# Eight-row edge steps for the last image, its four branch products taken two chunks at a time, the steps beside them dealt out by cost, and the last output strip in halves

## The chip, the cores and the metric

The kernel runs on one core of a Trainium2 chip. The metric is the device time of one execution in microseconds. TensorE is called PE here (its weight load PEld), VectorE DVE, ScalarE ACT, GpSimd POOL, and SyncE, which only issues transfers, SP.

## What is computed

The input `x` has shape (4, 512, 64, 64) in float32. Two layers follow each other.

Layer 0 is a multi-scale linear attention. It makes query, key and value by 1x1 products, adds a copy that went through a 5x5 depthwise convolution, attends within groups of eight channels, projects back to 512 channels, scales and shifts, and adds `x`. Its result is called `y` here. Layer 1 works on `y`:

```
sobel = sqrt(conv(y, SX)**2 + conv(y, SY)**2 + 1e-8)
lap   = abs(conv(y, LAP))
diag  = max(abs(conv(y, D1)), abs(conv(y, D2)))
grad  = sqrt(sobel**2 + lap**2 + 1e-8)
ef    = gelu(scale * (w_branch[k] @ E[k]) + shift)    for the four maps E[k], 128 channels each
att   = sigmoid(w_att2 @ gelu(w_att1 @ mean(ef)))     the mean is over all pixels
z     = w_fuse @ (ef * att) + b
out   = gelu(layernorm over channels(z)) + y
```

The attention vector `att` of an image needs every `ef` of that image, so no fuse step of an image can start before its last branch product is through.

## The kernel before, in words

The images are worked on one after the other. Each image is cut into four groups of heads for layer 0, and the code for a group emits its steps from a list written out by hand. What is left of an image, called its stages, is written as three Python generators that emit a piece of work and then yield:

- `project_out` (lines 608 to 666): the final product of layer 0. For each of eight strips of 512 pixels and each of four chunks of 128 channels it loads `xr`, multiplies eight 128x512 tiles `hd` by weights `fold_sb` (L655), adds shift and `xr` on DVE (L660), and stores to `y` in DRAM. That is 32 y steps per image; a strip holds every fourth row of one half of the image, so the first 16 steps give the upper half of `y`.
- `edge_branches` (L668): for 16 strips `u` of four rows, and for two pairs of chunks, `edges` loads `win` (two chunks, six rows with the halo, on SP's queue), and makes the four maps with eleven DVE instructions (L696 to L722) and four on ACT (Square L709, Abs L713, Square L719, Sqrt L723). `branches` multiplies two of the four maps, over all four chunks, into one PSUM bank (L730, 256 columns each), and ACT takes each result through Gelu with a sum over pixels into `pool_sb` (L737) and stores it to `ef` in DRAM from its own queue (L742). `win` has two buffers, `maps` three, `dv` one.
- `fuse_out` (L754): loads the fuse weights and their channel means (`wf_sb`, `wf_mean`, L765 to L771), then the attention vector (L777 to L798), then eight strips `j` of 512 pixels. `fuse` multiplies one output chunk (four matmuls of 512 columns, L808), ACT squares it (L810), DVE adds the bias to make `z` (L812), POOL sums the squares (L815). `norm` of the strip before multiplies by ones to sum over channels (`var`, L819), takes root (L821) and reciprocal (L822), and for each chunk loads `yr` (L826, two buffers), multiplies (DVE L829), takes Gelu (ACT L830), adds `y` (POOL L833) and stores (SP, L834). `z` has six buffers.

PSUM has two sets of four banks: the tag `ps` for ordinary products, and `quad` for four banks at once.

The order of the work on PE is that of emission. On the other engines a scheduler orders instructions; each engine's queue, SP's included, then runs in order. While the images before the last are worked on, `advance` emits the stages of the image before in proportion to estimated costs. After the last group of image 3 (the last image) nothing of layer 0 is left, and lines 940 to 956 emit the rest: the beginning of image 3's fuse stage (weights), 16 y steps of image 3, then one step of a list `rest` for each yield of image 3's edge stage. `rest` holds the second half of image 3's y steps and, after it, image 2's fuse stage. Last comes image 3's own fuse stage:

```python
    next(fused)
    next(edged)
    next(projected)
    ...
    for _ in range(NCH * NJ // 2):
        next(projected)
    rest = [projected] + behind
    for n, _ in enumerate(edged):
        while rest and next(rest[0], None) is None:
            rest.pop(0)
    for stage in rest + [fused]:
        for _ in stage:
            pass
```

Of the kernel before, what the change touches and what calls it, by code (L numbers as in the profile page):

```python
# [8 lines left out]
F32 = mybir.dt.float32  # L9
# [58 lines left out]
WAIT_Y, WAIT_E, WAIT_F = 32.0, 16.0, 26.0  # L68

# [14 lines left out]
def conv_seq_kernel(  # L84
# [582 lines left out]
    def edge_branches(b, efs, pool_sb, side):  # L667

        y = ys[b % 2]
        with ExitStack() as stack:  # L670
# [3 lines left out]
            share = SHARE_E / (2 * NJ * 4)  # L674

            slot = (2, 0, 1, 3)
            run = WB * 4 - 2
            yield 0.0

            def edges(u, pair):  # L680

                win = pool.tile([P, 2, 6 * WB], F32, name="win", tag="win")
                nc.sync.dma_start(
                    out=win,
                    in_=y[2 * pair : 2 * pair + 2].rearrange("c p r w -> p c (r w)")[:, :, 4 * u * WB : (4 * u + 6) * WB],
                )
                above, mid, below = (win[:, :, n * WB : (n + 4) * WB] for n in range(3))
                maps = pool.tile([P, 4, 2, 4 * WB], F32, name="maps", tag="maps", bufs=3)
# [4 lines left out]
                dv = pool.tile([P, 2, 2, 4 * WB], F32, name="dv", tag="dv", bufs=1)  # L693
# [8 lines left out]
                half = 2 * 4 * WB  # L702
# [22 lines left out]

            def branches(u, ks, maps):
                ps = ps_tile("br")
                for n, k in enumerate(ks):
                    for c in range(NCH):
                        nc.tensor.matmul(  # L730
                            rows(ps)[:, 4 * n : 4 * n + 4, :], lhsT=wbr_sb[:, k, c, :],
                            rhs=rows(maps[c // 2][:, slot[k], c % 2, :], WB)[:, :, 0:W],
                            start=(c == 0), stop=(c == NCH - 1),
                        )
                o = pool.tile([P, 2, 256], F32, name="ef_o", tag="ef_o")
                for n, k in enumerate(ks):
                    nc.scalar.activation(  # L737
                        o[:, n, :], ps[:, 256 * n : 256 * n + 256], AF.Gelu,
                        bias=shift1[:, k : k + 1], scale=scale1[:, k : k + 1], accum_out=pool_sb[:, k, u : u + 1],
                    )  # L740
                step = ks[1] - ks[0]
                nc.scalar.dma_start(  # L742
                    out=efs[u // 2][:, ks[0] : ks[1] + 1 : step, 256 * (u % 2) : 256 * (u % 2) + 256], in_=o
                )

            held = []
            for u in range(2 * NJ + 1):
                first = [edges(u, 0)] if u < 2 * NJ else []
                yield share if u else share + WAIT_E
                if held:  # L750
                    branches(u - 1, (1, 2), held)
                    yield share
                    branches(u - 1, (0, 3), held)
                    yield share  # L754
                if first:
                    held = first + [edges(u, 1)]
                    yield share if u else share + WAIT_E

    def fuse_out(b, efs, pool_sb, side):

        y = ys[b % 2]
        with ExitStack() as stack:
# [42 lines left out]
            def fuse(c, ef, zs, total):  # L805
                ps = ps_tile("zps")
                for k in range(4):
                    nc.tensor.matmul(ps, lhsT=wf_sb[:, k, ts(c, P)], rhs=ef[k], start=(k == 0), stop=(k == 3))  # L808
                sq = total if c == 0 else pool.tile([P, 512], F32, name="sq", tag="sq", bufs=3)
                nc.scalar.activation(sq, ps, AF.Square, bias=fbias[:, c : c + 1])  # L810
                z = pool.tile([P, 512], F32, name="z", tag="z", bufs=6)
                nc.vector.tensor_scalar(z, ps, fbias[:, c : c + 1], None, ALU.add)  # L812
# [4 lines left out]
            def norm(j, zs, total):  # L817
                ps = ps_tile("var")
                nc.tensor.matmul(ps, lhsT=ones, rhs=total, start=True, stop=True)  # L819
                rstd = pool.tile([P, 512], F32, name="rstd", tag="rstd", bufs=1)  # L820
                nc.scalar.activation(rstd, ps, AF.Sqrt, bias=ln_eps, scale=1.0 / C)  # L821
                nc.vector.reciprocal(rstd, rstd)  # L822
                for c in range(NCH):
                    z = zs[c]
                    yr = pool.tile([P, 8 * WB], F32, name="yr", tag="yr")
                    nc.sync.dma_start(  # L826
                        out=yr, in_=y[c].rearrange("p r w -> p (r w)")[:, (8 * j + 1) * WB : (8 * j + 9) * WB]
# [6 lines left out]
                    nc.sync.dma_start(out=out[b, c, :, ts(j, 512)], in_=z)  # L834

            held = None
            for j in range(NJ + 1):
                if j < NJ:
                    ef = []
                    for k in range(4):  # L840
                        t = pool.tile([P, 512], F32, name="ef", tag="ef", bufs=8)
                        nc.sync.dma_start(out=t, in_=efs[j][:, k, :])
                        ef.append(t)
                    zs = []
                    total = pool.tile([P, 512], F32, name="total", tag="total")
                    fuse(0, ef, zs, total)
                    yield share
                    fuse(1, ef, zs, total)
# [3 lines left out]
                if held:  # L852
                    norm(j - 1, *held)
                    yield share
                if j < NJ:
                    fuse(2, ef, zs, total)
                    yield share
                    fuse(3, ef, zs, total)
                    yield share
                    held = zs, total  # L860

    def stages(b, heads, cheads, folded, side="right"):

        efs = [dram.tile([P, 4, 512], F32, name=f"ef{j}") for j in range(NJ)]
        pool_sb = small.tile([P, 4, 2 * NJ], F32, name="pool_sb")
# [75 lines left out]
    next(fused)  # L941
# [6 lines left out]
    for _ in range(NCH * NJ // 2):  # L948
        next(projected)
    rest = [projected] + behind  # L950
    for n, _ in enumerate(edged):
        while rest and next(rest[0], None) is None:
            rest.pop(0)
    for stage in rest + [fused]:
# [97 lines left out]
```

## Time and profile before

| what | value |
|---|---|
| median of three timed runs | 5082.15 us (5077.47 to 5088.09) |
| profiled execution, its own time | 5063.71 us |
| profiled execution, its span | 5061.9 us |
| mean granted PE clock | 0.967 |
| PE busy | 4702.0 us (93%) |
| DVE busy | 2124.7 us (42%) |
| ACT busy | 1626.5 us (32%) |
| POOL busy | 392.7 us (8%) |
| DMA | 866.26 MB, mean 171 GB/s |

The span runs from the first to the last instruction of one execution that was traced. The groups of instructions on the page are named by line, engine, operation and tile. A float32 matmul is two records on PE, so the 1024 products of a line appear as x2048. The landmarks in the last part of the trace are these: image 3's first y step starts at 4341 us, the first edge instruction of image 3 on DVE at 4452.83, the last y step ends shortly before 4594, the last branch product of image 3 ends at 4905.15, its first fuse product starts at 4910.71, and the last `var` product at 5038.01.

### The profile page before, as it was taken

The page shows a single profiled execution, that of the slowest core. Times are in us where ns is not written, and L with a number is a line of the kernel's source. Part 1 is how long each engine was busy: PE and PEld are TensorE (multiplying, and loading weights), DVE is VectorE, ACT ScalarE, POOL GpSimd, SP SyncE. Part 2 cuts the span into 40 slices and gives each one's busy share as a digit, 9 for nine tenths or more (in the row PEclk, how much of TensorE's full clock was granted, in tenths as well). Part 3 has the DMA queues.
Part 4 walks back from the last instruction along what each step waited for, and adds up shares of the span by engine and source line. Part 5 has one row for each costly group of instructions (what it writes and reads, how often), then busy time and mean ns, then how long its engine had stood idle before and what let it go on. Part 6 is the DMA issues. An engine that isn't in the chain of part 4 may idle for free. (4 is left out here: it accounts for less than half of the span.)

```text
span 5061.9 us, 107134 instructions
## 1 busy us (share of the span) xinstructions
PE 4702.0 (93%) x46362; PEld 2739.7 (54%) x46362; DVE 2124.7 (42%) x2960; ACT 1626.5 (32%) x2833; POOL 392.7 (8%) x291
## 2 busy tenths in 40 slices
PE   9999999999999999799899999899989898898777
PEld 5665654455666554454465655454456665445443
DVE  1222221116556433211455653431146557157965
ACT  2112111004444423200345442320024445035765
POOL 0000000000000013100000000310000000001335
PEclk9999999999999999899999999999999999999889
DMA  6444466666656565676555665657655553774425
GB/s 196 138 123 130 132 206 190 158 165 181 192 189 183 179 205 170 197 178 156 176 176 181 193 202 176 213 188 167 163 173 175 184 169 129 200 184 118 151 88 172
DMA packets 635945, 866.26 MB, mean 171 GB/s; under 512 B 324393, under 2 KB 395081, under 8 KB 617041
## 3 DMA queue, kind: packets, MB, share of 16 engines
q1 hardware_dynamic: 551504, 758.68, 51.8%
q10 hardware_dynamic: 83968, 100.74, 6.4%
q8 instruction: 364, 5.96, 0.5%
q14 instruction: 109, 0.88, 0.1%
HBM read 578.09 MB, written 213.98 MB: 156 GB/s over the span
## 5 line engine op out<-in xcount | busy, mean ns | idle before, releaser
L262 PE MATMUL proj<-xt,w_sb 128*128 128x512 f32 x2048 | 955.8, 610 | 52.9 <-DMA xt<-in_x 31.8
L655 PE MATMUL yps<-hd,fold_sb 128*128 128x512 f32 x2048 | 899.6, 596 | 9.7 <-DMA hd<-heads 8.7
L396 PE MATMUL cv<-inp,mat 32*32 32x512 f32 x20480 | 730.2, 597 | 35.4 <-issue 27.3
L262 PEld LDWEIGHTS proj<-xt,w_sb 128*128 128x128 f32 x2048 | 382.7, 194 | 523.3 <-issue 450.7
L655 PEld LDWEIGHTS yps<-hd,fold_sb 128*128 128x128 f32 x2048 | 384.9, 190 | 493.5 <-issue 445.3
L396 PEld LDWEIGHTS cv<-inp,mat 32*32 32x32 f32 x20480 | 420.3, 103 | 314.6 <-issue 154.2
L730 PE MATMUL br<-maps,wbr_sb 128*128 128x256 f32 x2048 | 495.0, 396 | 51.8 <-ACT maps L713 42.2
L808 PE MATMUL zps<-ef,wf_sb 128*128 128x512 f32 x1024 | 469.9, 610 | 53.5 <-DMA ef<-ef 19.0
L730 PEld LDWEIGHTS br<-maps,wbr_sb 128*128 128x128 f32 x2048 | 399.7, 198 | 165.9 <-issue 51.3
L284 PEld LDWEIGHTS val<-w_sb,xt 128*128 128x128 f32 x4096 | 470.2, 192 | 33.9 <-issue 26.1
L284 PE MATMUL val<-w_sb,xt 128*128 128x128 f32 x4096 | 484.9, 277 | 0.6 <-DVE vt L291 0.3
L660 DVE SCALAR_TENSOR_TENSOR yt<-yps,shift,xr 128x512 f32<-128x512 f32 x128 | 96.1, 750 | 871.8 <-PE yps L655 788.9
L268 ACT COPY strip<-proj 128x512 f32<-128x512 f32 x256 | 149.1, 582 | 928.5 <-PE proj L262 910.4
L451 PE MATMUL corr<-near,ckt 128*32 128x160 f32 x8192 | 333.6, 315 | 35.0 <-DMA near<-near 28.4
L808 PEld LDWEIGHTS zps<-ef,wf_sb 128*128 128x128 f32 x1024 | 196.1, 195 | 296.6 <-issue 235.6
L241 POOL TENSOR_TENSOR mat<-dp_sb 128x1280 f32<-128x1280 f32 x32 | 77.2, 2414 | 3464.5 <-PE cv L396 2951.0
L451 PEld LDWEIGHTS corr<-near,ckt 128*32 128x32 f32 x8192 | 256.9, 111 | 131.5 <-issue 73.1
L703 DVE TENSOR_TENSOR maps<-dv 128x1054 f32<-128x1054 f32 x128 | 162.6, 1271 | 366.9 <-PE br L730 366.9
L312 ACT ACTIVATE kt<-tr 128x512 f32<-128x512 f32 x128 | 75.8, 593 | 528.9 <-PE tr L310 345.9
L737 ACT ACTIVATE ef_o<-br,shift,scale 128x256 f32<-128x256 f32 x256 | 142.3, 559 | 283.5 <-PE br L730 251.9
L360 DVE RECIPROCAL rec<-rec 128x512 f32<-128x512 f32 x64 | 214.4, 3350 | 1.7
L812 DVE TENSOR_SCALAR z<-zps,fbias 128x512 f32<-128x512 f32 x128 | 94.9, 744 | 283.4 <-DMA out<-z 97.0
(125 smaller groups left out, 4135.7 us busy)
## 6 DMA issues: line engine op xcount, KB each, us to landing
xt<-in_x SPq DMA_DIRECT2D x316, 512.0 KB
near<-near SPq DMA_DIRECT2D x512, 264.0 KB
inp<-strip ACTq DMA_DIRECT2D x1024, 64.0 KB
win<-y SPq DMA_DIRECT2D x128, 396.0 KB
near<-vt SPq DMA_DIRECT2D x512, 66.0 KB
y<-yt SPq DMA_DIRECT2D x128, 264.0 KB
yr<-y SPq DMA_DIRECT2D x128, 264.0 KB
heads<-q SPq DMA_DIRECT2D x128, 256.0 KB
```

Of the source, the lines that this page charges most:

```text
L262: nc.tensor.matmul(ps, lhsT=self.w[t][:, c, :], rhs=xs[self.b, j][c], start=(c == 0), stop=(c == NCH - 1))
L268: nc.scalar.copy(s, ps)
L284: nc.tensor.matmul(ps[:, ts(c, P)], lhsT=xs[self.b, j][n][:, ts(c, P)], rhs=self.w[VALUE][:, n, :], start=(n == 0), stop=(n == NCH - 1),)
L360: nc.vector.reciprocal(rec, rec)
L396: nc.tensor.matmul(rows(banks[i])[32 * j : 32 * j + 32, :, c0:c1], lhsT=self.mat[t][q, j, (dx + 2) * 8 + 4 * b : (dx + 2) * 8 + 4 * b + 4, :],
L451: nc.tensor.matmul(self.banks[jj][32 * i : 32 * i + 32, 160 * b : 160 * b + 160], lhsT=self.held["c", i][:, at : at + 32], rhs=v[:, 4 * n ...
L655: nc.tensor.matmul(ps, lhsT=fold_sb[g // NG][:, g % NG, ts(c, P)], rhs=hd[g], start=(g == 0), stop=(g == 2 * NG - 1),)
L660: nc.vector.scalar_tensor_tensor(yt[:, :, 1 : W + 1], rows(ps), shift0[:, c : c + 1], rows(xr), ALU.add, ALU.add)
L703: nc.vector.tensor_sub(flat[:, half : 3 * half - 2], dvs[:, 2 : 2 * half], dvs[:, 0 : 2 * half - 2])
L730: nc.tensor.matmul(rows(ps)[:, 4 * n : 4 * n + 4, :], lhsT=wbr_sb[:, k, c, :], rhs=rows(maps[c // 2][:, slot[k], c % 2, :], WB)[:, :, 0:W] ...
L737: nc.scalar.activation(o[:, n, :], ps[:, 256 * n : 256 * n + 256], AF.Gelu, bias=shift1[:, k : k + 1], scale=scale1[:, k : k + 1], accum_o ...
L808: nc.tensor.matmul(ps, lhsT=wf_sb[:, k, ts(c, P)], rhs=ef[k], start=(k == 0), stop=(k == 3))
```

## The change

The change touches only what is emitted after the last group, and the three stage generators.

1. For image 3 (`side == "left"`) the edge stage takes eight rows per strip: eight strips, two pairs of chunks each, 16 calls of `edges` with tiles twice as long. After each call its pair of chunks is multiplied at once: for all four maps, two chunks each, 512 columns, into four banks of the tag `quad`; the second pair of a strip closes the sums, and then ACT makes four Gelus of 512 columns and stores them in two transfers. The order on PE is: emit `edges(n)`, then other steps, then the products of `edges(n-1)`.
2. The other steps are dealt out by cost: each y step counts 6.9 us and each fuse step 2.95, and each pair of chunks is followed by 34 us of them the first time and an even share (11.76 us) afterwards; 18 us are kept for the time in which image 3's attention vector is made.
3. Image 2's attention vector is made among the first 16 y steps of image 3 (after steps 5, 9 and 13). Image 3's fuse weights are loaded when its y steps are through, not before them.
4. Image 2's `z` (b == B - 2) is made by ACT, not by DVE.
5. The last strip of image 3's fuse stage is worked on as two pieces of 256 pixels.

The rest of the diff only passes lengths through (`tall`, `wide`, `n`, `piece`) so that other images keep their four-row steps. Its core:

```diff
+            tall = 8 if side == "left" else 4
+            steps, wide = H // tall, tall * W
...
+            def product(ps, k, c, maps):
+                nc.tensor.matmul(
+                    rows(ps), lhsT=wbr_sb[:, k, c, :], rhs=rows(maps[:, slot[k], c % 2, :], WB)[:, :, 0:W],
+                    start=(c == 0), stop=(c == NCH - 1),
+                )
+
+            def store(u, ks, parts):
+                o = pool.tile([P, 2, wide], F32, name="ef_o", tag="ef_o")
+                for n, k in enumerate(ks):
+                    nc.scalar.activation(
+                        o[:, n, :], parts[n], AF.Gelu,
+                        bias=shift1[:, k : k + 1], scale=scale1[:, k : k + 1], accum_out=pool_sb[:, k, u : u + 1],
+                    )
+                at, step = wide * u % 512, ks[1] - ks[0]
+                nc.scalar.dma_start(out=efs[wide * u // 512][:, ks[0] : ks[1] + 1 : step, at : at + wide], in_=o)
...
+            if side == "left":
+
+                banks = None
+                for n in range(2 * steps + 1):
+                    made = edges(n // 2, n % 2) if n < 2 * steps else None
+                    yield 1.0
+                    if n:
+                        u, pair = divmod(n - 1, 2)
+                        if pair == 0:
+                            banks = quad_tiles("br")
+                        for k in (1, 2, 0, 3):
+                            for c in (2 * pair, 2 * pair + 1):
+                                product(banks[k], k, c, held)
+                        if pair:
+                            for ks in ((1, 2), (0, 3)):
+                                store(u, ks, [banks[k] for k in ks])
+                    held = made
+                yield 0.0
+                return
...
+            pieces = [(j, 0, 512) for j in range(NJ)]
+            if b == B - 1:
+                pieces[-1:] = [(NJ - 1, 0, 256), (NJ - 1, 256, 512)]
...
-                nc.vector.tensor_scalar(z, ps, fbias[:, c : c + 1], None, ALU.add)
+                z = pool.tile([P, 512], F32, name="z", tag="z", bufs=6)[:, :n]
+                if b == B - 2:
+                    nc.scalar.activation(z, ps, AF.Identity, bias=fbias[:, c : c + 1])
+                else:
+                    nc.vector.tensor_scalar(z, ps, fbias[:, c : c + 1], None, ALU.add)
...
-    next(fused)
     next(edged)
     next(projected)
...
-    for _ in range(NCH * NJ // 2):
+    for n in range(NCH * NJ // 2):
         next(projected)
-    rest = [projected] + behind
-    for n, _ in enumerate(edged):
-        while rest and next(rest[0], None) is None:
-            rest.pop(0)
-    for stage in rest + [fused]:
+        if n in (4, 8, 12):
+            next(behind[0])
+    rest, spent, given = [projected] + behind, 0.0, 0.0
+
+    def fill(much):
+
+        nonlocal spent, given
+        given += much
+        while rest and spent < given:
+            spent += FILL_Y if rest[0] is projected else FILL_F
+            if next(rest[0], None) is None:
+                if rest.pop(0) is projected:
+                    next(fused)
+
+
+    each = FILL_FIRST
+    for more in edged:
+        if not more:
+            break
+        fill(each)
+        each = FILL_EACH
+    for _ in range(3):
+        next(fused)
+        fill(FILL_ATT / 3)
+    for stage in rest + [fused, edged]:
         for _ in stage:
             pass
```

## The prediction

> **What bounds the kernel now.** I read first the engine rows in 40 slices of the page, where PE is full for most of the span and falls off in the last slices while DVE fills:
>
> ```profile
> PE   9999999999999999799899999899989898898777
> DVE  1222221116556433211455653431146557157965
> ```
>
> The chain of waits holds only the last 9 us, so I cut the end of the span into stretches: image 3's second half of y with its first edge strips (4459:4607), the remaining edge strips beside image 2's fuse steps (4607:4880), the drain and the attention vector (4880:4911), image 3's fuse steps (4911:5035), and the tail. Columns: length, then busy us and instruction count of PE, PEld, DVE, ACT, POOL, then clock, DMA share, GB/s.
>
> ```profile
> 4459.00:4607.00 148.00, 144.16 (x411) 77.38 (x410) 85.12 (x127) 62.90 (x84) 0.00 (x0) 0.98 0.68 166
> 4607.00:4880.00 273.00, 212.05 (x598) 124.47 (x598) 253.97 (x300) 202.66 (x277) 89.67 (x52) 0.89 0.41 127
> 4880.00:4911.00 31.00, 16.56 (x65) 13.48 (x64) 13.86 (x18) 21.26 (x33) 5.22 (x4) 0.72 0.25 85
> 4911.00:5035.00 124.00, 119.59 (x270) 50.72 (x269) 67.08 (x64) 59.84 (x75) 59.86 (x47) 0.99 0.49 153
> ```
>
> The first stretch is bound by PE (144 of 148) with DVE idle for 63 us; the second by DVE (254 of 273) with PE idle for 61; the third is a drain. The waits of PE from 4459 to 4911 say for whom (total, times, longest):
>
> ```profile
> PE br L730 <- ACT maps L713: 42.2, 8, 11.4
> PE zps L808 <- DVE z L812: 12.2, 3, 7.3
> PE zps L808 <- DVE wf_sb L797: 6.6, 2, 5.4
> ```
>
> The last link is named ACT, but behind the maps stands the full DVE. So one stage wastes DVE and the next wastes PE.
>
> **Prices.** In the PE timeline the matmuls run back to back:
>
> ```profile
> 4714.03 3.62 PE L730 MATMUL br<-maps,wbr_sb 128*128 128x256 f32 x16
> 4717.48 10.46 PE L808 MATMUL zps<-ef,wf_sb 128*128 128x512 f32 x24
> ```
>
> A 128x512 record costs 0.434 us (3.60 us to the next start for 8), a 128x256 one 0.226; every f32 matmul is two records. So a y step (8 matmuls) is 6.95 us, a fuse step (4) 3.48, its `var` 0.87, eight br matmuls of 512 columns 6.95. On DVE I take start-to-start times, since a duration overlaps the next start:
>
> ```profile
> 4712.19 1.25 DVE L703 TENSOR_TENSOR maps<-dv 128x1054 f32<-128x1054 f32 x1
> 4713.36 0.69 DVE L706 SCALAR_TENSOR_TENSOR maps<-win,maps 128x524 f32<-128x524 f32 x1
> 4713.98 0.69 DVE L717 TENSOR_TENSOR maps<-dv 128x526 f32<-128x526 f32 x1
> ```
>
> That is 1.17 us for 1054 elements and 0.62 for 524: 1.04 ns per element and 0.07 fixed. ACT the same way: 0.97 for 1048 elements, 0.53 for 524, so 1.85 for 2096, and 2.05 for the Sqrt.
>
> **Part 1, eight-row edge steps.** Before: 32 half steps of 10 x 0.62 + 1.17 = 7.35 us of DVE. After: 16 steps of 10 x 1.17 + 2.26 = 13.9. That saves 0.8 x 16 = 12 us of DVE, no more: the fixed cost is small. The br matmuls go from 512 records of 256 columns (138.1 us busy in the trace, 116 if dense) to 256 of 512 columns, 111 us. ACT per step: 0.97 + 1.85 + 1.85 + 2.05 = 6.7, and half as many table switches. Loads of `win` and stores of `ef` halve in number on SP's and ACT's queues; the bytes of `win` shrink with the halo.
>
> Against this speaks the Trainium skill (Perfetto Trace Analysis, Optimizing Scalar/DVE Operations): where Scalar or Vector is not saturated but causes bubbles on others, break instructions up. By it, the 5.3 us mean wait of PE for maps would double: if all 8 waits stay, 42 us more, over half of the gain that follows. But in the stretch where those waits are, DVE is busy 93%, so the condition does not hold; the larger step is filled over on PE (part 2). I take nothing, and keep 42 us for a rival.
>
> **Part 2, products at once, other steps dealt out.** The product of each pair of chunks needs one pair's maps. It accumulates in four banks of its own, a new wait: the first product of a strip waits for the previous strip's four Gelus on ACT (one Gelu 0.78 us, a table load 1.29), and behind it on PE stand the fuse steps. In the built order 11.8 us of fill stands between (except once, between products 5 and 6, where maps are old); nothing up to 11.8 us, the excess beyond. The fills are 5 y steps, then 2, 2, 2, 1, 2, 2, 0, then about four fuse steps each.
>
> PE from T0 = 4459, the end of the 16th y step (its eviction starts at 4459.06): 16 x 6.95 = 111 of y, 16 x 6.95 = 111 of br, 120 of image 2's 128 fuse matmuls x 0.87 = 104, six `var` 5; sum 332. That is PE's bound for the end of the last product.
>
> DVE: edge step n needs one of three `maps` buffers, so product n-3 done. Adding up PE's order, products 4 and 5 end at T0+132 and +153. Step 7 thus runs T0+132 to 146; step 8 starts at 146 and waits 3.5 us for a buffer. From there: 8 x 13.9 = 111; five of image 2's norms, which stand ahead of the last edge step in the built order, 5 x (3.34 + 4 x 0.87) = 34 (L822's mean, and L829's 0.96 in that stretch less the overlap); the weight mean of `next(fused)`, now in mid-stage, 2048 elements, 2.1; contention with POOL. For the last: the 21 half steps of the second stretch cost (254 - 75.5 of L812, L829, L822, L797)/21 = 8.5 instead of 7.35, 24 us by 52 POOL instructions; 35 of these give 16. Sum 163; at the 254 of 273 that DVE reached before, 175. So DVE ends at T0+146+3.5+175 = +324.5. The last step's exposed ACT square 3, Sqrt with table load 3.3, product 7: T0+338, 4797. DVE and PE are now nearly level; before, that product ended at 4905.
>
> **Part 3, z of image 2 on ACT.** It takes 32 x 0.66 = 21 us off DVE (L812's 0.73 less the overlap; already left out above) and puts 30 x 0.57 = 17, the pace of L810, on ACT in the late half. ACT there: 8 x 6.7 + 20 Gelus x 0.78 + 60 evictions x 0.57 + 6 x 0.58 + 24 x 0.71 + 14 table loads (counted in the built order) x 1.29 = 142 us of some 185. The page ScalarE: Activation LUTs (What ACT_TABLE_LOAD costs) speaks against it: each switch 1283 ns and a drain of 1380. The row shows the load, and the next activation 1.29 us after its start:
>
> ```profile
> 4713.60 1.28 ACT L737 ACT_TABLE_LOAD   x1
> 4714.89 0.56 ACT L737 ACTIVATE ef_o<-br,shift,scale 128x256 f32<-128x256 f32 x1
> ```
>
> So no drain beyond it is seen. By the page ACT would need 142 + 14 x 1.38 = 161 us, still under 185. I take 142. Queued behind a waiting zps eviction on ACT are the next edge activations; four banks, 14 us of PE work, cover that.
>
> **Part 4, attention steps.** Image 2's two small products (0.63 + 1.05 us in the trace at 4597) move before T0, among y steps: +2 us on T0; the 5.4 us wait for `wf_sb` and the ones beside it go (PE is the bound there afterwards, counted in the 332). Image 3's weights load (1.3 MB on SP) moves from the start to after the last y store, ahead of the second `win` of the fifth strip; that win is needed only after DVE's 14 us of step 8: nothing, 0 to 6. Image 3's attention chain: product end to first zps was 4910.71 - 4905.15 = 5.6 us; now image 2's last two fuse steps lie in it (7.8 us), and its last norms stand before Sigmoid on DVE and ACT; I take 16 (12 to 22).
>
> First zps: 4813, 98 us before 4910.7.
>
> **Part 5, last strip in halves.** PE +0.5. The tail hangs on SP and two `yr` buffers:
>
> ```profile
> 5026.93 1.13 PE L819 MATMUL var<-total,ones 128*128 128x512 f32 x2 [0.46 <-DVE z L812]
> ...
> 5053.18 0.92 SPq L826 DMA_DIRECT2D yr<-y  x2
> 5056.55 2.30 POOL L833 TENSOR_TENSOR z<-z,yr 128x512 f32<-128x512 f32 x2 [3.78 <-issue]
> ```
>
> Each pair of chunks costs one round of load (3.4 us) and POOL (2.3). Halving shortens the reciprocal by 1.7, POOL by 1.2 per pair, and DVE and ACT by about 2, but adds a norm, so two more rounds of about 4 us, and z's six buffers wait for stores of the strip before. Gain 5, loss 5 to 8: I take 1.5 us lost, from -6 to +8.
>
> **Sum.** 98 - 2 - 1.5 = 94 us. The profiled span 5061.9 becomes 4968; its execution took 5063.71 (1.8 us around the span), so 4970. The median of the three timed runs is 5082.15, 18 above; I subtract the same 94: **4988**.
>
> **Rivals.**
> - *PE alone bounds* (0.15): DVE loses nothing to waits, the product ends at the 332, six us earlier, and the tail gains 6 where I took a loss of 1.5: about 4975. For it: PE's clock was 0.89 in the second stretch and 0.98 to 0.99 where it is full. Against: three engines at 77 to 95% seldom mesh.
> - *The bubbles stay* (0.17): each late step still costs PE the 5.3 us that a wait for maps costs now, 8 x 5.3 = 42: 5030. For it: ACT's strict order mixes edges, evictions and Gelus. Against: a step now has a fill of 11.8.
> - *Slower* (0.05): the four br banks become the lock. If the Gelus of a strip stand on ACT behind all of the next edge step, and the evictions with them, PE idles a DVE step of about 22 us less one product of 7 per strip: 8 x 15 = 120 us lost, 5108. It decides from 94/8 = 11.8 us per strip on. Against: in the built order the Gelus follow one Sqrt at most.
> - The balance as worked out: 0.63.
>
> **How the numbers follow.** The measurement tells about 0.2% (10 us) from no change. Range 4966 to 5032: the first rival, part 5's gain, the ends of parts 4 and 5 below and above, and the 42 us. Only a loss of over 84 us makes it "same": 0.02 between bubble and lock. Faster 0.94, slower 0.04.
>
> **What would show it.** DVE in the second half of image 3's edges busy over 90% beside PE over 85% at a clock near 1; br 256 records, about 111 us; DVE's edge steps near 14 us before POOL works and 16 after; waits of br for maps under 25 us; the first zps of image 3 near 4813; the tail from the last full `var` longer than 35 us. I am wrong if br waits long for `ef_o` Gelus, or ACT passes 90% there.

## The result, and the profile after

The changed kernel takes 5020.18 us (median of four runs, 5005.83 to 5033.35) against 5080.17 (5077.47 to 5088.09): ratio 0.988, 95% interval 0.9867 to 0.9893. The gain is 60 us; 94 were predicted. The time lies inside the range, 32 us above the number.

The profiled execution is the slowest of the four: 5033.35 us, span 5031.6. It reaches image 3's first y step at 4362.7, before's at 4341.4, although the code up to there does the same work; over the thirteen kernels traced after the change the point lies between 4338.0 and 4365.2. So stages are counted from that y step, called y0 below. From y0 to the end: 720.5 us before, 668.9 after.

| us from y0 | before | after | term of the sum |
|---|---|---|---|
| PE ends the 16th y step (T0) | 116.5 | 123.9 | 117.6 + 2 predicted, 4.3 late |
| first edge product starts | 139.0 | 178.4 | |
| last edge product ends | 563.8 | 494.8 | T0+338 predicted, T0+370.9 |
| image 3's first fuse step | 569.3 | 509.0 | 16 us later predicted, 14.3 |
| end | 720.5 | 668.9 | 152.7 us later predicted, 159.8 |

The prediction took for T0 the start of that step's eviction on DVE, 1.1 us behind PE's end. The misses are 4.3 + 32.9 - 1.7 + 7.1 = 42.6 us, which to 0.2 us is the difference between 94 and 51.6.

PE and DVE in 40 slices, from the page of the changed kernel:

```profile
PE   9999999999999999799899999989999899899887
DVE  1222222115565533311355553441125555447955
```

The hole in the last slices of PE is smaller, and DVE's block is shorter. The same stretches as before, cut at the changed kernel's own points: from T0 to the first late fill, the late half of the edges, the attention vector, image 3's fuse steps, and the tail. Columns: length, then busy us and count of PE, PEld, DVE, ACT, POOL, then clock, DMA share, GB/s.

```profile
4486.00:4643.00 157.00, 152.87 (x352) 66.56 (x351) 124.33 (x106) 71.72 (x59) 0.00 (x0) 0.99 0.62 153
4643.00:4858.00 215.00, 191.71 (x418) 82.25 (x417) 178.15 (x117) 147.66 (x179) 85.91 (x46) 0.93 0.48 155
4858.00:4872.00 14.00, 10.32 (x36) 4.84 (x35) 7.13 (x10) 10.21 (x15) 4.81 (x4) 0.91 0.20 75
4872.00:4991.00 119.00, 109.39 (x253) 48.01 (x254) 69.39 (x65) 64.72 (x82) 63.83 (x50) 0.97 0.57 175
4991.00:5032.00 41.00, 16.92 (x54) 12.24 (x54) 18.17 (x24) 17.96 (x26) 16.97 (x19) 0.71 0.43 129
```

In the first stretch DVE now works 124 of 157 us beside a full PE; before it idled there for 63 of 148. In the second no engine is full: PE 89%, DVE 83%, ACT 69%. The waits of PE over both (total, times, longest):

```profile
PE var L864 <- ACT z L853: 16.0, 3, 7.4
PE var L864 <- POOL total L858: 5.4, 1, 5.4
PE yps L661 <- DMA hd<-heads: 4.1, 2, 3.7
PE zps L848 <- ACT z L853: 1.9, 3, 1.2
```

The 42.2 us of `br` waiting for maps are gone. In their place stand 21.4 us at `var`, the small product with which a fuse strip makes its variance (before the change it waited 3.4 us there). Beside them PE's own work is 344.6 us busy where 332 were reckoned (br 116.1 for 256 records, y 113.8, zps 109.2, `var` 11.0; they overlap a little). 344.6 + 27.4 idle = 372. Part of the excess is slow work right behind a wait: the four `var` that waited take 2.05 to 2.08 us, the two that did not 1.02.

A `var` needs two things. One is the strip's sum of squares, which ACT and then POOL make. The other is a free bank of the tag `ps`: there are four, and a strip takes five in turn (four `zps`, one `var`). ACT empties a bank by taking the square and `z` from it. `var` reads no `z`, so the row "`var` <- ACT z", 16.0 of the 21.4 us, is a wait for a bank. PE, ACT and POOL around the second of the four waits (start, us, engine, line, operation; idle before and its releaser in brackets):

```profile
4763.92 2.08 PE L864 MATMUL var<-total,ones 128*128 128x512 f32 x2 [3.91 <-ACT z L853]
```

```profile
4758.76 2.93 ACT L876 ACTIVATE z<-z,vec_sb 128x512 f32<-128x512 f32 x4
...
4763.18 0.69 ACT L853 ACTIVATE z<-zps,fbias 128x512 f32<-128x512 f32 x1 [0.16 <-DMA out<-z]
```

```profile
4751.52 2.62 POOL L858 TENSOR_TENSOR total<-total,sq 128x512 f32<-128x512 f32 x2 [12.82 <-ACT sq L850]
```

The sums were through at 4754.14. The `z` that empties the bank stood on ACT behind four Gelus, waited 0.16 us for the store of an earlier `z`, and ended at 4763.87; `var` starts at 4763.92. At 4795.51 it is the same; at 4707.45 sum and `z` end within 1 us of each other. Only the last of the four waits, 5.40 us, is for the sum. The timelines of PE and ACT around it:

```profile
4809.98 10.46 PE L848 MATMUL zps<-ef,wf_sb 128*128 128x512 f32 x24
4825.84 2.07 PE L864 MATMUL var<-total,ones 128*128 128x512 f32 x2 [5.40 <-POOL total L858]
4827.71 9.19 PE L738 MATMUL br<-maps,wbr_sb 128*128 128x512 f32 x16
4836.74 13.90 PE L848 MATMUL zps<-ef,wf_sb 128*128 128x512 f32 x32
4850.47 7.03 PE L738 MATMUL br<-maps,wbr_sb 128*128 128x512 f32 x16
```

```profile
4818.02 1.08 ACT L720 ACTIVATE lap<-maps 128x1052 f32<-128x1052 f32 x1
...
4819.14 1.96 ACT L724 ACTIVATE maps<-maps 128x2104 f32<-128x2104 f32 x1
4821.00 1.94 ACT L730 ACTIVATE maps<-maps 128x2104 f32<-128x2104 f32 x1
4822.85 0.67 ACT L850 ACTIVATE sq<-zps,fbias 128x512 f32<-128x512 f32 x1
```

PE has the last of the strip's `zps` ready at 4820.4. Its square stands on ACT behind 5 us of an edge step's activations and starts at 4822.85; POOL's last sum follows, from 4823.65 to 4825.8, and `var` starts at 4825.84. All that stands behind `var` on PE is late with it: the product of step 14, then 14 us of fill, then the last product at 4850.47. DVE's last edge instruction had begun at 4824.70 and ended at 4826.9, 23.6 us before that product began. The prediction put 6.3 there.

### The profile page after: what moved, and what is told of

The parts are those of the page before. It is cut to its first block, busy times and chain, and to the rows that moved or that the text cites. A ratio compares the mean times of both kernels' runs of the same rounds, so it can differ in the third digit from the quotient of the medians.

```text
span 5031.6 us, 106279 instructions
## 1 busy us (share of the span) xinstructions
PE 4694.3 (93%) x46140; PEld 2689.2 (53%) x46140; DVE 2083.3 (41%) x2761; ACT 1581.8 (31%) x2712; POOL 397.3 (8%) x298
## 5 line engine op out<-in xcount | busy, mean ns | idle before, releaser
L661 PE MATMUL yps<-hd,fold_sb 128*128 128x512 f32 x2048 | 907.8, 599 | 18.5 <-DMA hd<-heads 16.2
L848 PE MATMUL zps<-ef,wf_sb 128*128 128x512 f32 (+1 forms) x1056 | 473.4, 601 | 36.4 <-DMA ef<-ef 19.4
L738 PE MATMUL br<-maps,wbr_sb 128*128 128x256 f32 (+1 forms) x1792 | 474.2, 418 | 3.7 <-DVE s_sb L335 2.9
L738 PEld LDWEIGHTS br<-maps,wbr_sb 128*128 128x128 f32 x1792 | 340.9, 193 | 146.9 <-issue 102.0
L457 PE MATMUL corr<-near,ckt 128*32 128x160 f32 x8192 | 333.7, 315 | 40.3 <-DMA near<-near 32.9
L714 DVE TENSOR_TENSOR maps<-dv 128x1054 f32<-128x1054 f32 (+1 forms) x112 | 158.0, 1411 | 376.3 <-PE br L738 376.2
L746 ACT ACTIVATE ef_o<-br,shift,scale 128x256 f32<-128x256 f32 (+1 forms) x224 | 131.4, 590 | 228.1 <-PE br L738 210.4
L415 ACT ACTIVATE co<-cv 128x256 f32<-128x256 f32 x256 | 94.0, 398 | 331.1 <-PE cv L402 310.6
```

What stands on the lines that cost most here:

```text
L457: nc.tensor.matmul(self.banks[jj][32 * i : 32 * i + 32, 160 * b : 160 * b + 160], lhsT=self.held["c", i][:, at : at + 32], rhs=v[:, 4 * n ...
L661: nc.tensor.matmul(ps, lhsT=fold_sb[g // NG][:, g % NG, ts(c, P)], rhs=hd[g], start=(g == 0), stop=(g == 2 * NG - 1),)
L714: nc.vector.tensor_sub(flat[:, half : 3 * half - 2], dvs[:, 2 : 2 * half], dvs[:, 0 : 2 * half - 2])
L738: nc.tensor.matmul(rows(ps), lhsT=wbr_sb[:, k, c, :], rhs=rows(maps[:, slot[k], c % 2, :], WB)[:, :, 0:W], start=(c == 0), stop=(c == NCH ...
L746: nc.scalar.activation(o[:, n, :], parts[n], AF.Gelu, bias=shift1[:, k : k + 1], scale=scale1[:, k : k + 1], accum_out=pool_sb[:, k, u : u ...
```

## The experiments

All of them are edits of the changed kernel, run once each, e12 five times; the numbers are us from y0 of each run's own trace.

| run | last product ends | image 3's first fuse step | end | from there to the end |
|---|---|---|---|---|
| changed kernel | 494.8 | 509.0 | 668.9 | 159.8 |
| e1_z8_image2 | 489.7 | 504.5 | 662.2 | 157.7 |
| e2_z_on_dve | 488.8 | 504.1 | 663.9 | 159.7 |
| e3_last_strip_whole | 488.7 | 502.9 | 655.0 | 152.0 |
| e4_four_rows | 493.9 | 506.7 | 675.6 | 168.8 |
| e5_four_per_step | 527.9 | 532.8 | 691.0 | 158.2 |
| e6_z8_yr4_image2 | 489.1 | 504.7 | 663.7 | 159.0 |
| e7_no_sums_image2 | 470.9 | 486.7 | 645.6 | 158.9 |
| e8_first_fill_20 | 493.2 | 507.5 | 665.8 | 158.2 |
| e9_fewer_dve | 482.7 | 497.0 | 654.5 | 157.5 |
| e10_no_late_fill | 466.7 | 479.5 | 660.5 | 181.0 |
| e11_tail_buffers | 483.8 | 498.1 | 639.9 | 141.8 |
| e12_together | 466.6 | 479.5 | 649.6 | 170.2 |

e3 and e11 run the changed kernel's order up to image 3's first fuse step, and end the last product at 488.7 and 483.8; so 484 to 495 is what that order gives, and smaller differences in this column say nothing. Counted from the first product instead of y0, most of the spread goes: that stretch takes 316.4 us in the changed kernel, 314.0 in e3, 314.3 in e11.

### Dealing out, row height, halves and z, each undone

**e5_four_per_step.** The other steps four at a time again:

```
-        given += much
-        while rest and spent < given:
-            spent += FILL_Y if rest[0] is projected else FILL_F
-            if next(rest[0], None) is None:
+        for _ in range(4):
+            if rest and next(rest[0], None) is None:
```

Expected:

> The changed kernel with the dealing by cost undone: after each eight-row half step four of the other steps are emitted, whatever they cost, which is what the kernel before did (one after each of its yields). The y steps are then through after four half steps and image 2's fuse steps begin there. Theory (dealing out carries the gain): PE full and DVE waiting first, DVE full and PE waiting later, as before the change; last br product 530 to 550 us after the first y step of image 3, where the changed kernel in the runs so far has 489 to 495. Rival (the products two chunks at a time carry it, since PE no longer needs both pairs of maps): 490 to 505.

Measured: last product 527.9, 33 to 39 us later than in the changed kernel, e1, e2 and e6 (7 of them are two more fuse steps that stand ahead of it), and the end 22 to 29. The total is 5050.40 (before on this chip: 5068.72). Dealing out carries about half of the 52 to 58 us that lie between these ends and before's 720.5. The late stretch (from 4617 to 4886) is again as full of DVE as before the change:

```profile
4617.00:4886.00 269.00, 219.19 (x481) 94.27 (x479) 247.90 (x160) 190.81 (x224) 109.77 (x56) 0.90 0.45 145
```

DVE is busy for 248 of 269 us. PE waits 27.7 us at `var` and 21.1 at `br`; the other steps are used up at 4834, and the last two edge products wait 11.1 us and, in two halves, 5.7 and 4.3, with nothing left to fill.

**e4_four_rows.** Four-row edge steps with everything else kept:

```
-            tall = 8 if side == "left" else 4
+            tall = 4
```

Expected:

> The changed kernel with four-row steps for image 3 too, all else as changed: 16 strips, br products of 256 columns, the shares of the other steps halved. Theory: the rows are the small part: 12 us more of DVE and 5 of PE, last br product 5 to 20 us later than 494.6 after the first y step of image 3. Rival 1 (eight rows carry the gain): 40 us or more later. Rival 2 (the shorter step lets PE and ACT mesh better): earlier.

Measured: last product 493.9, end 675.6, total 5024.79. Beside e1, e2 and e6 (663.3 on average) eight rows are worth 12 us at the end. The last products can't be compared: with the shares halved, 28 of image 2's fuse steps stand ahead of it here and 30 there. In the late stretch, from 4640 to 4850, `br` waits again for maps, and now for its banks:

```profile
PE br L738 <- ACT ef_o L746: 15.0, 4, 7.9
PE br L738 <- ACT maps L734: 11.9, 3, 6.2
PE var L864 <- ACT z L853: 7.9, 2, 4.0
```

So the 12 us are not just the 12 us of DVE time that was reckoned; that the two agree may be chance.

**e2_z_on_dve.** Image 2's z on DVE again:

```
-                if b == B - 2:
-                    nc.scalar.activation(z, ps, AF.Identity, bias=fbias[:, c : c + 1])
-                else:
-                    nc.vector.tensor_scalar(z, ps, fbias[:, c : c + 1], None, ALU.add)
+                nc.vector.tensor_scalar(z, ps, fbias[:, c : c + 1], None, ALU.add)
```

Expected:

> The changed kernel with image 2's z made by DVE, as before the change (part 3 undone). Theory: DVE has 21 us more in a half where it is busy 90%, and the wait for z's stores now stands in DVE's queue ahead of edge instructions; the last br product ends 10 to 25 us later than the 494.6 us after the first y step of image 3. Rival (moving z to ACT was the mistake, since ACT's queue then holds the edge activations back): it ends 10 to 20 us earlier.

Measured: last product 488.8, end 663.9, total 5011.75: no difference from e1 and e6. From 4464 to 4835 DVE works 314.3 us (e1, from 4464 to 4836: 304.0), and nothing moves. So DVE had that much room.

**e3_last_strip_whole.** Part 5 undone:

```
-            if b == B - 1:
-                pieces[-1:] = [(NJ - 1, 0, 256), (NJ - 1, 256, 512)]
```

Expected:

> The changed kernel with the last strip of image 3 in one piece (part 5 undone). In the changed kernel image 3's fuse stage lasts 160 us from its first product to the end, before the change 151. Theory (halves cost: one more norm with its rounds of yr loads, and z's six buffers wait for stores of the strip before): 151 to 154. Rival (halves help, the stage is long for another reason, such as image 2's last norms beside it): 163 to 166.

Measured: from image 3's first fuse step to the end 152.0 us, against 157.5 to 159.8 with halves (before: 151.2). Halving costs 6 to 8 us. The timeline of PE in the changed kernel shows where: the last whole strip and both halves wait. The last `var` starts 141.4 us behind image 3's first fuse step, in e3 127.9; the end comes 18.4 us behind it, in e3 24.2.

```profile
4990.76 2.07 PE L864 MATMUL var<-total,ones 128*128 128x512 f32 x2 [4.13 <-DVE z L855]
...
5004.63 0.70 PE L864 MATMUL var<-total,ones 128*128 128x256 f32 x2 [3.32 <-DVE z L855]
...
5013.18 0.70 PE L864 MATMUL var<-total,ones 128*128 128x256 f32 x2 [1.49 <-POOL total L858]
```

### What makes `var` wait

**e1_z8_image2.** ACT's z waits 18.0 us for the stores of the six z buffers. Two more for image 2:

```
-                z = pool.tile([P, 512], F32, name="z", tag="z", bufs=6)[:, :n]
+                z = pool.tile([P, 512], F32, name="z", tag="z", bufs=8 if b == B - 2 else 6)[:, :n]
```

Expected:

> The changed kernel with eight z buffers in place of six for image 2 alone. Measured in the trace from the start of image 3's first y step, the changed kernel ends its last br product after 494.6 us and waits on ACT 18 us for z's stores. Theory (z's buffers): the waits of var and zps for ACT's z (18 us) and ACT's wait for the stores fall under 5 us, PE's idle time in the late half falls from 23 to under 10, and the last product ends after 470 to 480 us. Rival 1 (three nearly full engines in a fixed order don't mesh): the waits go to other links, the last product stays within 5 us of 494. Rival 2 (DVE slowed by POOL's instructions): DVE's busy time in the late half stays and so does the end.

Measured: last product 489.7, 317.3 us behind the first one: nothing gained. The wait for stores went, and another took its place (PE, 4625 to 4836):

```profile
PE var L864 <- POOL total L858: 22.5, 2, 16.3
PE zps L848 <- ACT z L853: 7.3, 3, 4.9
```

The wait is as long and now for the sum instead of the bank. Behind the longest of these waits stands ACT again: the strip's `zps` is ready at 4788.8, ACT takes its square at 4802.59, behind Gelus and two activations of an edge step with 3.1 us idle between them, and POOL's sum follows at 4803.40. The theory that the z buffers hold the product falls.

**e6_z8_yr4_image2.** The same with four `yr` buffers for image 2, so that POOL does not stand in a residual add that waits for its load.

Expected:

> The changed kernel with eight z and four yr buffers for image 2. With eight z buffers alone ACT's wait for stores fell from 18 us to nothing, but 22 us of PE waits for POOL's sums took its place. Theory P (POOL's queue: the sums of the next strip stand behind the four adds of y of this one, of which two wait for yr): PE's wait for POOL falls under 8 us and the last br product comes 10 to 20 us earlier, at 470 to 480. Rival D (DVE, 94% busy until its last edge step, sets the pace, and PE's waits only take up the slack): within 5 us of 489, the wait again elsewhere.

Measured: 489.1. POOL no longer waits for `yr` (12.2 us in e1), and `var` waits 22.5 us for POOL as in e1. This falls too.

**e8_first_fill_20.** `FILL_FIRST` 20 instead of 34 us, so that edge products start earlier and DVE gets its buffers back sooner.

Expected:

> The changed kernel with a first fill of 20 us in place of 34, the rest dealt out evenly, so that the first products come 14 us earlier and free the maps buffers earlier: DVE waits 26 us for them in the first half. Theory D (DVE bounds from there on): DVE runs ahead by up to 14 us and the last br product comes 8 to 14 us earlier than 489. Rival (PE and the fuse chain bound): within 4 us of 489.

Measured: the first product starts at 159.6 instead of 169 to 178, and DVE ends its last edge instruction at 451.5 instead of 455 to 464 (changed kernel, e1, e3, e11); the last product ends at 493.2 all the same. An earlier DVE did not help.

**e7_no_sums_image2.** Leaves out POOL's 24 additions of squares for image 2; `var` then needs only the first square, which ACT writes.

```
-                if c:
+                if c and b != B - 2:
```

Expected:

> The changed kernel without POOL's 24 sums of squares for image 2, so that its layernorm sees one chunk in four (part of the computation is left out). Takes 24 of some 46 POOL instructions out of the late half. Theory D (DVE sets the pace, and each POOL instruction that meets a two-input DVE instruction holds it up by about 1 us): DVE's edge step falls from 17.5 to about 16, DVE's last edge instruction and the last br product come 10 to 20 us earlier. If only PE's wait for the sums counted, DVE's step would stay at 17.5 and only the 5 to 7 us of that wait would go.

Measured: last product 470.9, 294.8 us behind the first one instead of 314 to 317. Its late half and PE's waits there, and the same of e3, which keeps the sums:

```profile
4645.00:4836.00 191.00, 181.04 (x412) 78.49 (x411) 163.25 (x117) 143.34 (x172) 42.26 (x24) 0.98 0.52 170
PE var L864 <- ACT z L853: 3.9, 2, 2.0
```

```profile
4634.00:4843.00 209.00, 184.69 (x409) 79.53 (x408) 175.46 (x117) 145.60 (x174) 92.72 (x46) 0.94 0.48 157
PE var L862 <- ACT z L851: 12.1, 3, 7.0
PE var L862 <- POOL total L856: 7.1, 1, 7.1
```

The stretch is 18 us shorter; PE idles 10 us instead of 24 and is busy for 4 less at a clock of 0.98 instead of 0.94. At `var` 3.9 us of waits are left of 19.2, and not only the sum's 7.1 went, but 8.2 of the bank's 12.1 as well. ACT's `z` still waits 19.9 us for stores (16.7 in e3), so earlier stores are not the reason. DVE is 12 us less busy for the same 117 instructions; it meets 22 POOL instructions fewer. Its edge step takes 16.1 us (17.6 in e3), and its last edge instruction ends 271.7 us behind the first product (284.4 in e3), as the theory of a tax on DVE had it. Two readings are left: the sums as a link of the path to `var`, or the sums as a tax on DVE.

**e9_fewer_dve** is to tell them apart. It leaves out one of DVE's two instructions for `sv` in the 16 steps, and keeps POOL's work:

```
-                nc.vector.scalar_tensor_tensor(sv, dvs[:, 1 : half - 1], 2.0, sv, ALU.mult, ALU.add)
+                if side == "right":
+                    nc.vector.scalar_tensor_tensor(sv, dvs[:, 1 : half - 1], 2.0, sv, ALU.mult, ALU.add)
```

Expected:

> Leaves out, for image 3's 16 edge steps, the second of the two DVE instructions that build sv (one of ten of 1.17 us, so the output differs); POOL's work stays. Measured from the start of image 3's first y step (y0). If DVE with POOL's contention is what sets the last product, it ends 10 us earlier (8 late steps x 1.2 to 2.3 less what the first half cannot use): about y0+478 instead of y0+488 to 494, and DVE's last edge instruction near y0+450. If the chain of evictions and fuse steps on PE, ACT and POOL sets it, the product stays at y0+486 to 490 though DVE ends its edges earlier, as in the run with a first fill of 20. Image 3's first fuse step 14 us behind the product either way.

Measured: DVE has 161.1 us of work in the late half (4619 to 4822), eleven less than e11 in its own (171.8 from 4617 to 4822). The last product comes 313.3 us behind the first, against 314.3 in e11 and 314.0 in e3. PE's waits are what they were:

```profile
PE var L865 <- ACT z L854: 17.4, 3, 8.0
PE zps L849 <- ACT z L854: 3.9, 3, 2.1
PE var L865 <- POOL total L859: 3.4, 1, 3.4
```

DVE's last edge instruction does not even end earlier: 285.8 us behind the first product, in e11 285.3. DVE now waits 15.6 us for ACT's `maps`, so it follows. Eleven us less DVE bring 1 us, the sums 19. With e2 (ten us more, no loss) that speaks against DVE as the bound: neither less nor more work on it moved the product. It does not shut the tax out, since in e7 DVE's edge work did end earlier and here it did not. The better reading is the path from a strip's `zps` over ACT (squares and `z`) and POOL (sums) to `var`, with the edge products queued behind `var`. Which link of it counts is not separated: e7 takes out POOL's time and the need for three of four squares at once.

**e10_no_late_fill.** If the last product is late because fuse steps stand ahead of it, they can be put behind it (last strip whole here, so e3 is the comparison):

```
-    for more in edged:
+    for n, more in enumerate(edged):
...
-        fill(each)
+        fill(each if n < NJ * 2 - 1 else 0.0)
```

Expected:

> Last strip whole, and no other steps dealt out after the product before the last one, so that the last products follow each other on PE and the fuse steps that stood between move behind them, into the attention chain. If the 23 us from DVE's last edge instruction to the last product are fill and evictions that stand ahead of it, the last product starts near y0+467 instead of y0+482 and ends near y0+474. What is moved (up to eight fuse steps, 28 us of PE) then stands in the attention gap: image 3's first fuse step at y0+493 to 498 instead of 503 if the gap grows from 14 to about 22; if all of it has to be done before the attention vector matters, it stays at 503 and only the order has changed. Tail 152.

Measured: the last product ends at 466.7, 22 us earlier than in e3, and the first fuse step after the attention products starts at 479.5; yet the end is at 660.5, 5.5 us later than e3's. Seven fuse steps, 24 us of PE, were moved: 23 stand ahead of the last product instead of 30, and six of image 2's come behind the attention products. `var` waits 15.0 us as it did (19.2 in e3). So what was moved is paid for behind: 181.0 us instead of 152.0. From 4780 on PE's timeline shows the price of the products without fill:

```profile
4798.88 7.12 PE L738 MATMUL br<-maps,wbr_sb 128*128 128x512 f32 x12 [2.81 <-ACT ef_o L746]
4810.31 6.67 PE L738 MATMUL br<-maps,wbr_sb 128*128 128x512 f32 x8 [4.32 <-ACT maps L734]
```

PE stands for its banks and for maps where it had worked on fuse steps. Counted from the first product, 8.2 us are lost by the end (488.5 against 480.3).

**e11_tail_buffers.** Last strip whole, and for image 3 eight z and four yr buffers:

```
-                z = pool.tile([P, 512], F32, name="z", tag="z", bufs=6)[:, :n]
+                z = pool.tile([P, 512], F32, name="z", tag="z", bufs=8 if b == B - 1 else 6)[:, :n]
...
-                    yr = pool.tile([P, 8 * WB], F32, name="yr", tag="yr")[:, : high * WB]
+                    yr = pool.tile([P, 8 * WB], F32, name="yr", tag="yr", bufs=4 if b == B - 1 else 2)[:, : high * WB]
```

Expected:

> Last strip whole, image 3 with eight z buffers and four yr buffers. If the tail waits for buffers (z for the stores of the strip before, yr for POOL), the time from image 3's first fuse step to the end falls from 152 to about 145 us. If the rounds of load, POOL and store bound it by their own length, it stays at 151 to 153. Everything up to image 3's first fuse step as with the whole strip: last product y0+489, first fuse step y0+503.

Measured: 141.8 us to the end, ten fewer than e3. PE's timeline of e3, then of e11:

```profile
4925.77 1.13 PE L862 MATMUL var<-total,ones 128*128 128x512 f32 x2 [1.34 <-DVE z L853]
...
4942.02 1.12 PE L862 MATMUL var<-total,ones 128*128 128x512 f32 x2 [0.48 <-DVE z L853]
```

```profile
4902.72 1.12 PE L862 MATMUL var<-total,ones 128*128 128x512 f32 x2
4903.68 13.90 PE L846 MATMUL zps<-ef,wf_sb 128*128 128x512 f32 x32
4917.41 1.12 PE L862 MATMUL var<-total,ones 128*128 128x512 f32 x2
...
4932.30 1.12 PE L862 MATMUL var<-total,ones 128*128 128x512 f32 x2
```

A strip takes 16.2 us there and 14.7 to 14.9 here, PE's own work. What DVE's `z` waits for in image 3's fuse stage is a buffer whose store has to land; the rows of the kernel before, of e3 and of e11:

```profile
DVE z L812 <- DMA out<-z: 37.0, 21, 4.1
DVE z L853 <- DMA out<-z: 35.0, 19, 4.3
DVE z L853 <- DMA out<-z: 1.0, 2, 0.6
```

So image 3's fuse steps were held by buffers, and by the first row they were before the change too. The rows point to `z`; `yr` was changed with it, and the two were not tried apart. The total is 4979.72 us in one run, 0.982 of the 5069.56 (nine runs) of before on that chip.

**e12_together.** e10 and e11 in one, in five runs.

Expected:

> The three together: last strip whole, no fill after the product before the last, eight z and four yr buffers for image 3. If they add up, 8 us of the halved strip, 5 to 10 of the last products and up to 7 of buffers come off the changed kernel's time: 0.984 to 0.985 of the time before, against 0.988 for the change as it is. If the moved fuse steps and the buffers bring nothing, only the whole strip counts: 0.9865.

Measured: 4999.01 us (4982.59 to 5017.59), ratio 0.9864, interval 0.984 to 0.9889, which overlaps the changed kernel's own. Its trace ends 478.8 us behind the first product, e11's 470.4: the missing fill costs 8.4 us here and 8.2 between e10 and e3. By the traces e11 is the better version, but there is one run of it, and its 4979.72 is hardly below the lowest of e12's five.

## Why the prediction was right or wrong

**Right.** The sign, nearly two thirds of the size, and where the gain lies: DVE's edge work moves under image 3's y steps, and both the wait of `br` for maps and the last product's lateness fall. An edge step with nothing on POOL takes DVE the 13.9 us reckoned, and `br` is 256 records (116.1 us busy, 111 reckoned from one start to the next). The rule of the Trainium skill (Perfetto Trace Analysis, Optimizing Scalar/DVE Operations) that speaks for smaller steps did not apply: with the whole change the waits for maps went from 42.2 us to none; with four rows alone undone 11.9 came back (e4), with the dealing out alone undone 10.0 (e5). The table load still takes 1.28 us (14 of them in the late half), and ACT, at 69%, had the room that was reckoned. The attention vector took 14.3 us for 16.

**Luck.** That the time lies inside the range is in part luck. Its upper end, 5032, was set by 42 us of waits for maps; these did not come, and 42.6 us were lost elsewhere.

**Wrong: T0+338.** The step that failed is the end of the last product, T0+370.9, 33 of the 42.6 us. It was the sum of DVE's work up to its end, then 13.5 us for ACT and the product. Two of its terms were off, and by the runs only one of them counted:

- DVE's end. POOL's contention was sized at 16 us; a late step takes 17.9 us instead of 13.9 (138.5 us for 85 instructions, eleven a step), so 8 x 4.0 = 32. DVE ended at T0+340.3 instead of +324.5. But in e8 DVE ended 3 to 13 us earlier and the product did not follow, and in e9 less work on DVE moved neither, so no run shows that this error cost anything by itself.
- Behind DVE, 13.5 us were set, and 30.6 measured. The prediction made PE's queue free of waits except at `br`: it charged a strip's `var` with 0.87 us of work and looked at POOL as a tax on DVE only. In the runs that keep eight rows, dealing out, late fill and sums `var` waits 19 to 23 us in all, for its bank or for its sum, with edge products behind it. Leaving out POOL's sums brings the product 19 to 23 us forward, counted from the first one (e7 against the changed kernel, e1 and e3); buffers and DVE's load do not (e1, e2, e6, e9). The bank was no term of the prediction: it looked at four banks as a cover for ACT's waits. PE's work beside it was 344.6 us, not 332, in part from work behind a wait: the edge products at 4709.29 and 4827.71 take 8.67 and 9.19 us with a clock of 0.76 and 0.71, others 7.03 with 1.00.

Of the signs named, three did not come in the late half: DVE over 90% (83%), edge steps near 16 us (17.9), a clock near 1 (0.93).

The prediction's first rival, PE alone as the bound, would have needed `var` without waits. The rival of staying bubbles gave 5030, which is nearer to the measured time than the forecast, but its mechanism, waits for maps, is not there.

**Wrong: part 5.** -1.5 us was taken, and it costs 6 to 8 (e3). The waits for z's buffers were named and priced too low: the fuse stage was already waiting for buffers, as e11 shows with 10 us. With halves PE's `var` waits 11.1 us for DVE's `z` in image 3's stage, with the whole strip 3.0. Halves with more buffers were not tried.

**Part 3** was reckoned as a gain of 21 us on DVE; it changes nothing (e2). **Part 2**'s dealing out is worth about half of the 52 to 58 us (e5: 22 to 29 us at the end), **part 1** about 12 (e4). Beside e1, e2 and e6 that leaves 57 - 28 - 12 + 7 for the halves = 24 us, if the parts add at all. The product of each pair of chunks at once and **part 4** were not tried alone, so whose they are stays open.

**T0** on PE was 7.4 us later in the profiled run than before the change (123.9 against 116.5), not 2. Image 2's attention products take the 0.63 and 1.05 us reckoned. Behind y0 PE waits 1.9 us for loads of `hd` before the change, 3.9 after, 3.4 in e3 and 1.4 in e11, where the step ends at 117.1. Behind the longest of these waits in the changed kernel, 2.57 us before 4397.26, the clock is 0.60 up to 4404, in other stretches of these steps 1.00. So most of the excess goes with the spread of the loads.

**The working.** The prices of PE were a little high and the forecast did not hang on it: sixteen 256-column records start 3.45 us before the next row in the line shown, which is 0.216 each and not 0.226, and 32 records of 512 columns take 13.73 us to the next start (4836.74 to 4850.47), 0.429 each and not 0.434. By these part 1 saves PE nothing (110.4 against 109.9 us), where 5 were reckoned. And 42 us are less than half of 94, not over half.

**Open:** how much of the path to `var` is ACT's order (squares and `z` behind edge activations), how much the four banks and how much POOL's own time. e7 takes out the sums and the need for the later squares together, so that DVE's earlier end there may have a share, and no run has more banks for `zps` and `var`.

## What to carry to other kernels

A small matmul that needs a result of two other engines and a bank that one of them has to empty is a lock for everything behind it on PE: charge it with the whole way through those engines' queues, not with its own length. Read the releaser's name together with what the waiting instruction uses: here "ACT z" stood for a bank. When a buffer seems to be what is waited for, add one and see whether the wait goes or only moves to another link; here it moved for image 2, and went for image 3. Work moved from under a stage to behind it is not saved, and the fill that delays a last step may be what pays for its wait.

## What was not expected of the hardware

POOL and DVE hold each other up by about a whole instruction. In the timelines of the changed kernel, DVE and then POOL:

```profile
4801.43 2.23 DVE L728 TENSOR_TENSOR maps<-dv 128x1054 f32<-128x1054 f32 x1
4803.57 1.24 DVE L717 SCALAR_TENSOR_TENSOR maps<-win,maps 128x1052 f32<-128x1052 f32 x1
4804.74 2.31 DVE L729 SCALAR_TENSOR_TENSOR maps<-dv,maps 128x1054 f32<-128x1054 f32 x1
```

```profile
4798.71 3.83 POOL L879 TENSOR_TENSOR z<-z,yr 128x512 f32<-128x512 f32 x2 [3.92 <-DMA yr<-y]
4803.98 1.96 POOL L858 TENSOR_TENSOR total<-total,sq 128x512 f32<-128x512 f32 x1 [1.44 <-ACT sq L850]
```

DVE instructions of one length take 1.24 us or 2.2 to 2.3 (L728 and L729 take 1.25 where POOL has nothing), and one sum on POOL 1.26 (seen with DVE idle) or 1.96 to 2.2: the one that comes second pays about the other's length. That is what the Trainium skill (SBUF — State Buffer, Who interferes with whom) says of a DVE instruction with two inputs in SBUF beside a POOL instruction that reads SBUF. In the late half of e7, with 22 POOL instructions fewer than in e3's, DVE was 12 us less busy: half a microsecond for each.
